# Unread products, later due times and norms on VectorE in an attention layer with masks and residual norms

## The chip, the core and the metric

The kernel runs on one core of one Trainium2 chip. The metric is the time of one execution on the device in microseconds; the time of a kernel is the median of its runs. The engines are called PE (TensorE), DVE (VectorE), ACT (ScalarE), POOL (GpSimd) and SP (SyncE, which here only issues DMAs); PEld is PE's loading of weights.

## The reference

`x` is 8 frames of 2048 nodes with 256 channels, `adj` a 2048 x 2048 matrix of integers; all is float32.

```
def ln(x, g, b): return (x - mean(x)) * rsqrt(var(x) + 1e-5) * g + b      # over the 256 channels
q, k, v  = split(x @ w_qkv)                 # 8 heads of 32 channels
scores   = q . k / sqrt(32);  scores = where(adj > 0, scores, -1e9)
t        = softmax(scores) @ v
x1       = ln(x + t, ln1_g, ln1_b)
h        = relu(x1 @ w1 + b1)
x2       = ln(x1 + h @ w2 + b2, ln2_g, ln2_b)
out      = (x + x2 - mean) / sqrt(var + 1e-5)
```

So every row passes three norms: after attention, after the feed-forward part, and after the outer residual.

## The kernel before

**Items.** The work is a list of 1024 items (L658): 8 frames f, 4 chunks qc of 512 queries, 2 groups g of 4 heads, 16 blocks mb of 128 keys. One step t of the main loop (L733) does, in this order: side jobs (`advance`, L626), the exponential of item t + 1 on ACT (L283), the scores of item t + 2 (L276 on PE, and on DVE the addition of the mask, L279, which moves them from PSUM into a tile `p`), the values product of item t (L310 on PE), and the share of item t in the softmax sums (`add_up`, L324). There are 12 tiles `p`. Scores lie in three pairs of PSUM banks. Of the two other banks one gathers the values of a group, and the other serves the side jobs, one at a time.

**Softmax sums.** The 16 exponentials of a group are added up in three or four chains: some on POOL (L339, 4.9 us each), some by accumulating DMAs that POOL issues (L336); the heads of the chains are then multiplied with ones on PE (`denominator`, L367, product L383 "halves"), one chain head after the other, and may wait for late ones. After the second group the sums are turned (L393) and inverted, and `outcome` (L402) turns the attention output, multiplies it, and has x added by a DMA.

**Tails.** Ten steps later the chunk's `tail` (L435) starts: the first norm, the feed-forward part (`feed_forward`, L571: turn, w1 in two sets of two products, w2 in two), second norm, scale and shift on POOL (L445, L447), addition of x by DMA (L450), third norm, write to `out` (L453). A norm (L344) is statistics on DVE (L348, L349), the root on POOL (L353 to L357) and one activation per 256 channels on ACT (L360). The parameter `per` tells how many of a chunk's four row groups are treated per step. The chunk before the last has x loaded ahead (`xb`): PE adds it (L414), and at the end POOL does (L447).

**The planner.** Side jobs are generators in `fill`, sorted by their due step. A job yields a number of steps to sleep, or BANK before it takes the PSUM bank, or MORE between two sets of products for the same bank (and then keeps the bank). Sets cost credit: 4 x columns each, so 2048 for a set of four products of 512 columns; each step grants 2200, and at most 2200 is kept. `more()` lets a job go on while 1024 of credit is left, or if the due step of a waiting or holding job has been reached:

```
due = [e[3] for e in fill if e[2] == BANK and e[0] <= t or e is state["holder"]]
return finish or state["credit"] >= UNIT or min(due) <= t
```

So a step takes one set, and more than one only if a job is overdue. The other jobs are loading and turning x, the projections to q, k and v of the next frame, and in the first frame the masks.

**The ending.** The last group of the last chunk is done in two halves of 256 queries (L257, L290). `closing(h)` (L473) sums the exponentials of half h (L494), turns sums and attention output, and does the tail of its 256 queries itself: statistics (L456), norms (L467: a small product on DVE, two activations on ACT), feed-forward, norms, write (L569). `closing(0)` is due at step 1024, `closing(1)` at 1023. After the last item the planner runs everything to its end (L778).

After that, a check of all sums (L975 to L988) decides whether a general path is taken; here it isn't.

Of the kernel before, what the change touches and what calls it, by code (L numbers as in the profile page):

```python
# [61 lines left out]
def fast_path(ctx, tc, cst, x, adj, out, RS):  # L62
# [339 lines left out]
    def outcome(f, qc):  # L402
        yield ROOM
        state["tails"] += 1
        xin = x[f, qc * CH:(qc + 1) * CH, :].rearrange("(p j) c -> p j c", p=P)
        y = yp.tile([P, TPC, C], F32, name="y")
        begin = items.index((f, qc, 1, LAST)) + SUM + 2
        yield from divide(f, qc, y)
        if (f, qc) == (F - 1, NCK - 2):
            xb = state["xb"]  # L410
            for j in range(0, TPC, 2):
                yield BANK
                ps = bank()
                columns(ps, ident, xb[:, j:j + 2, :].rearrange("p j c -> p (j c)"), start=True, stop=True)  # L414
                nc.vector.tensor_tensor(y[:, j:j + 2, :], ps.rearrange("p (j c) -> p j c", c=C), y[:, j:j + 2, :], ALU.add)
            start(begin + 4, tail(f, qc, y, xin, 2, xb), begin + 18)
            return
        nc.gpsimd.dma_start(y, xin, accum_op=ALU.add)
        if (f, qc) == (F - 1, NCK - 3):
            start(begin + 10, tail(f, qc, y, xin, 2), begin + 18)  # L420
        else:
            start(begin + 10, tail(f, qc, y, xin), begin + 26)

    def divide(f, qc, y):
        rc = RC.pop((f, qc))
# [9 lines left out]
    def tail(f, qc, y, xin, per=1, xb=None):  # L435
        yield from norm(y, per)
        yield from feed_forward(y)
        if xb is not None:
            nc.gpsimd.tensor_tensor(xb, xb, rows(cst["be2r"]), ALU.add)
        yield 1  # L440
        z = y
        yield from norm(z, per if per == 1 else TPC)
        while xb is None and per > 1 and state["now"] % MB not in CALM:
            yield 1
        nc.gpsimd.tensor_tensor(z, z, rows(cst["g2r"]), ALU.mult)  # L445
        yield 1
        nc.gpsimd.tensor_tensor(z, z, rows(cst["be2r"]) if xb is None else xb, ALU.add)  # L447
        yield 1
        if xb is None:
            nc.gpsimd.dma_start(z, xin, accum_op=ALU.add)  # L450
            yield 7 if per == 1 else 10
        yield from norm(z, per)
        nc.sync.dma_start(out[f, qc * CH:(qc + 1) * CH, :].rearrange("(p j) c -> p j c", p=P), z)  # L453
        state["tails"] -= 1

    def half_stats(t):  # L456
        mv = small.tile([P, 2, nc.vector.BN_AGGR_DIM], F32, name="mv")
        for j in range(2):
            st = small.tile([P, nc.vector.BN_STATS_DIM], F32, name="st")
            nc.vector.bn_stats(st, t[:, j, :])  # L460
            nc.vector.bn_aggr(mv[:, j, :], st)
        rs = small.tile([P, 2], F32, name="rs")
        nc.gpsimd.tensor_scalar(rs, mv[:, :, 1], EPS, 1.0, op0=ALU.add, op1=ALU.mult)
        nc.gpsimd.tensor_tensor(rs, rs, cst["mhalf"][:, 0:2], ALU.pow)
        return mv, rs

    def half_norm(t, mv, rs):  # L467
        nb = small.tile([P, 2], F32, name="nb")
        nc.vector.scalar_tensor_tensor(nb, mv[:, :, 0], -1.0, rs, op0=ALU.mult, op1=ALU.mult)
        for j in range(2):  # L470
            nc.scalar.activation(t[:, j, :], t[:, j, :], AF.Identity, bias=nb[:, j:j + 1], scale=rs[:, j:j + 1])

    def closing(h):  # L473
        f, qc, g = ENDING
        own, part, t0 = slice(2 * h, 2 * h + 2), slice(h * HQ, (h + 1) * HQ), len(items) - MB // 2 * (2 - h)
        terms = [(5, 6), (1, 7), (0, 7), (6, 8), (7, 8)]
        dst = out[f, qc * CH + h * HQ:qc * CH + (h + 1) * HQ, :].rearrange("(p j) c -> p j c", p=P)

        def row2(v):
            return v[:, None, :].to_broadcast([P, 2, C])  # L480

        yield BANK
        ps = bank()
        for n, (block, when) in enumerate(terms):
            if n:
                yield MORE
            while state["now"] < t0 + when:
                yield WAIT
            term = PT.pop((*ENDING, block + h * MB // 2))
            state["credit"] -= 4 * CH  # L490
            for b in range(2):
                for i in range(4):
                    r = D * i
                    nc.tensor.matmul(ps[r:r + D, 0:HQ], cst["halves"][:, g, :], term[:, i, b * HQ:(b + 1) * HQ],  # L494
                                     start=(n + b == 0), stop=(n + b == len(terms)))
        dT = DT[f, qc]
        nc.vector.tensor_tensor(dT[:, part], ps[:, 0:HQ], dT[:, part], ALU.add)
        if h == 0:
            state["y"] = yp.tile([P, TPC, C], F32, name="y")
            state["ff"] = [work.tile([P, 2, CH], F32, name=n) for n in ("turned", "hT")]  # L500
        y, (yT, hT) = state["y"][:, own], state["ff"]
        xr, xb = (t[:, own] for t in state["rows"])
        def turned_sums():
            ps = bank()
            transposes(ps, [dT[:, part][:, j::2] for j in range(2)])
            den = ps[:, 0:HQ].rearrange("p (j c) -> p j c", c=P)[:, :, ::D // 2]
            rc = op.tile([P, 2, H], F32, name="rc")
            nc.vector.reciprocal(rc, den)
            return rc, den

        def count(den):
            nc.vector.tensor_tensor(RS[:, 0, own], RS[:, 0, own], den, ALU.add)
            nc.vector.tensor_tensor(RS[:, 1, own], RS[:, 1, own], den, ALU.min)

        yield 1
        if h == 0:
            yield BANK
            rc, den = turned_sums()
            count(den)
        yield BANK  # L520
        po = bank()
        transposes(po, [OT[f, qc, gg][:, part][:, j::2] for gg in range(2) for j in range(2)])
        if h:
            rc, den = turned_sums()
        for gg in range(2):
            nc.vector.tensor_tensor(y[:, :, gg * P:(gg + 1) * P].rearrange("p j (h d) -> p j h d", d=D),
                                    po[:, gg * HQ:(gg + 1) * HQ].rearrange("p (j h d) -> p j h d", h=4, d=D),
                                    rc[:, :, gg::2, None].to_broadcast([P, 2, 4, D]), ALU.mult)
        nc.vector.tensor_tensor(y, y, xr, ALU.add)
        found = half_stats(y)  # L530
        if h:
            count(den)
        yield 1
        half_norm(y, *found)
        nc.gpsimd.tensor_tensor(xr, y, row2(cst["g1r"]), ALU.mult)
        nc.gpsimd.tensor_tensor(xr, xr, row2(cst["be1b2r"]), ALU.add)
        yield BANK
        ps = bank()
        transposes(ps, [y[:, j, a * P:(a + 1) * P] for a in range(2) for j in range(2)])
        for a in range(2):  # L540
            nc.scalar.activation(yT[:, a, part], ps[:, a * HQ:(a + 1) * HQ], AF.Identity,
                                 bias=cst["be1c"][:, a:a + 1], scale=cst["g1c"][:, a:a + 1])
        yield 1
        for d in range(2):
            yield BANK
            ps = bank()
            for a in range(2):
                columns(ps[:, 0:HQ], w1s[:, a, d * P:(d + 1) * P], yT[:, a, part], start=(a == 0), stop=(a == 1))
            nc.scalar.activation(hT[:, d, part], ps[:, 0:HQ], AF.Relu, bias=cst["b1s"][:, d:d + 1], scale=1.0)
        yield 1  # L550
        yield BANK
        ps = bank()
        for j in range(2):
            if j:
                yield MORE
            for d in range(2):
                columns(ps[:, j * C:(j + 1) * C], hT[:, d, part][:, j * P:(j + 1) * P], w2s[:, d, :], start=(d == 0), stop=(d == 1))
        z = y
        nc.vector.tensor_tensor(z, ps.rearrange("p (b c) -> p b c", c=C), xr, ALU.add)
        found = half_stats(z)  # L560
        yield 1
        half_norm(z, *found)
        yield 1
        nc.vector.tensor_tensor(z, z, row2(cst["g2r"]), ALU.mult)
        nc.vector.tensor_tensor(z, z, xb, ALU.add)
        found = half_stats(z)
        yield 1
        half_norm(z, *found)
        nc.sync.dma_start(dst, z)  # L569
# [40 lines left out]
    def start(t, gen, due):  # L610
        fill.append([t, gen, 1, due])
        fill.sort(key=lambda e: e[3])
# [408 lines left out]
```

## Time and profile before

| | |
|---|---|
| median of 3 runs | 3159.01 us (3158.67 to 3160.27) |
| profiled execution | 3158.02 us |
| its span, first to last instruction | 3156.0 us |
| mean granted PE clock | 0.994 |
| busy: PE / DVE / POOL / ACT | 97% / 87% / 86% / 77% |
| exponential of 128 x 2048 (L283) | 1.910 us |
| mask addition of 128 x 1024 (L279), two per step | 1.218 us |
| POOL addition of 128 x 2048 (L339) | 4.890 us |
| DMAs: accumulating p (L336), issue to landing | 9.1 us median, 7.0 to 15.5 |

All times inside the run are microseconds from the first instruction of the span. In a row of the timeline the first number is the start, the second the time to the end of the last instruction that the row takes together, x the number of instructions (PE executes each float32 product as two), and in brackets stands the idle time of the engine before it and what ended it. A group's row shows line, engine, operation, output and inputs, their shapes, the count, then total busy time in us and the mean in ns, and the idle time before with its causes. The granted clock is the share of PE's full clock.

### The profile page before, as it was taken

The numbers are of one execution on the slowest core, as the hardware profiler recorded it, in microseconds if no ns is written. First come the engines' busy times: TensorE is split into PE (matmuls) and PEld (weight loads), VectorE is DVE, ScalarE is ACT, GpSimd is POOL, SyncE is SP. The second block draws the span as 40 slices with busy tenths as digits, with TensorE's granted clock in tenths as the row PEclk, the third lists the DMA queues.
The fourth block names the chain that finished last, engine by engine and source line by source line (L and its number), as shares of the span: only waits on it lengthen the run. The fifth ranks groups of instructions, "written<-read, shape, count | busy, mean of one in ns | idle before, by whom it ended". The sixth has DMA issues, their size and how long they took to land.

```text
span 3156.0 us, 68508 instructions
## 1 busy us (share of the span) xinstructions
PE 3051.3 (97%) x28988; PEld 962.6 (31%) x28988; DVE 2747.6 (87%) x3139; ACT 2427.1 (77%) x1934; POOL 2727.7 (86%) x1389
## 2 busy tenths in 40 slices
PE   8999999999999999999999999999999999999986
PEld 4222333233332233223332323323333233322223
DVE  4989888998888988888988888988888988889885
ACT  4877878777778877778777878778778778778774
POOL 1768989888889888899888899899989899899985
PEclk9999999999999999999999999999999999999998
DMA  8998878889789888789878899788888889778871
GB/s 258 223 210 185 196 170 194 193 191 198 173 174 209 197 190 178 170 195 214 192 169 187 187 207 195 166 184 204 197 176 191 190 192 202 167 173 166 173 157 42
DMA packets 165465, 586.86 MB, mean 186 GB/s; under 512 B 15360, under 2 KB 84480, under 8 KB 116512
## 3 DMA queue, kind: packets, MB, share of 16 engines
q0 software_dynamic: 63696, 430.60, 69.4%
q1 hardware_dynamic: 100640, 150.50, 14.1%
q8 instruction: 229, 3.75, 0.5%
q10 hardware_dynamic: 816, 1.31, 0.1%
q14 instruction: 84, 0.69, 0.1%
HBM read 146.15 MB, written 37.75 MB: 58 GB/s over the span
## 4 chain that ended last, share of the span: by engine, by line


## 5 line engine op out<-in xcount | busy, mean ns | idle before, releaser
L279 DVE TENSOR_TENSOR p<-s,mask 128x1024 f32<-128x1024 f32 x2016 | 2371.5, 1218 | 297.7 <-PE s L276 123.4
L283 ACT ACTIVATE p<-p 128x2048 f32<-128x2048 f32 x1024 | 1955.7, 1910 | 551.1 <-DVE p L279 449.1
L339 POOL TENSOR_TENSOR p<-p 128x2048 f32<-128x2048 f32 x409 | 1999.9, 4890 | 221.3 <-ACT p L283 200.4
L276 PE MATMUL s<-qT,kT 32*128 32x512 f32 x8064 | 1152.0, 640 | 56.5 <-DVE p L279 52.6
L310 PE MATMUL x<-p,v 128*32 128x512 f32 x8064 | 1075.8, 606 | 5.8 <-ACT p L283 4.2
L276 PEld LDWEIGHTS s<-qT,kT 32*128 32x128 f32 x8064 | 315.3, 183 | 659.5 <-DVE p L279 629.4
L336 POOL DMA_DIRECT2D p<-p x378 | 416.2, 1104 | 49.2 <-ACT p L283 41.0
L310 PEld LDWEIGHTS x<-p,v 128*32 128x32 f32 x8064 | 158.7, 108 | 771.3 <-issue 315.1
L54 PE MATMUL x<-in,wqkv 128*32 128x512 f32 x1888 | 245.7, 592 | 0.0
L383 PE MATMUL x<-p,halves 128*32 128x512 f32 x1768 | 231.1, 594 | 1.6 <-DVE kT L170 1.4
L360 ACT ACTIVATE y<-y,nb,rs 128x256 f32<-128x256 f32 x372 | 218.3, 591 | 0.5 <-POOL nb L357 0.5
L348 DVE BATCH_NORM_STATS2 st<-y 128x6 f32<-128x256 f32 x372 | 154.8, 416 | 0.0
L54 PE MATMUL x<-turned,w1s 128*32 128x512 f32 (+1 forms) x1008 | 125.2, 593 | 0.0
L54 PEld LDWEIGHTS x<-wqkv,in 128*32 128x32 f32 x3584 | 102.4, 110 | 66.5 <-issue 55.4
L54 PE MATMUL x<-w2s,hT 128*32 128x256 f32 x2048 | 122.0, 379 | 0.0
L54 PE MATMUL x<-wqkv,in 128*32 128x128 f32 x3584 | 118.2, 273 | 0.0
L54 PEld LDWEIGHTS x<-in,wqkv 128*32 128x32 f32 x1888 | 61.3, 110 | 141.3 <-issue 116.0
L354 POOL TENSOR_TENSOR rs<-rs,mhalf 128x4 f32<-128x4 f32 x93 | 96.2, 1035 | 7.8
L445 POOL TENSOR_TENSOR y<-y,g2r 128x1024 f32<-128x1024 f32 x31 | 99.3, 3205 | 2.2 <-ACT y L360 2.2
L383 PEld LDWEIGHTS x<-p,halves 128*32 128x32 f32 x1768 | 57.3, 110 | 133.9 <-issue 126.5
L447 POOL TENSOR_TENSOR y<-y,be2r 128x1024 f32<-128x1024 f32 x30 | 94.4, 3145 | 0.2
L54 PEld LDWEIGHTS x<-w2s,hT 128*32 128x32 f32 x2048 | 66.4, 110 | 69.7 <-issue 35.6
(164 smaller groups left out, 1433.6 us busy)
## 6 DMA issues: line engine op xcount, KB each, us to landing
p<-p POOLq DMA_DIRECT2D x380, 1024.0 KB, 9.1
in<-xd SPq DMA_DIRECT2D x87, 512.0 KB, 7.5
mask<-md SPq DMA_DIRECT2D x248, 128.0 KB, 5.4
y<-in_x_dram POOLq DMA_DIRECT2D x60, 512.0 KB, 10.3
out_dram<-y SPq DMA_DIRECT2D x31, 512.0 KB, 4.5
in<-in_x_dram SPq DMA_DIRECT2D x30, 512.0 KB, 6.8
xd<-in SPq DMA_DIRECT2D x28, 512.0 KB, 6.8
p<-in_adj_dram SPq DMA_DIRECT2D x8, 1024.0 KB, 14.3
```

The costliest lines, as they stand in the source:

```text
L54: nc.tensor.matmul(out[r:r + D], lhsT[:, r:r + D], rhs, start=start, stop=stop)
L276: nc.tensor.matmul(ps2[half][:, j, :], KT[f, mb // TPC, g][r:r + D, (mb % TPC) * P:(mb % TPC + 1) * P], QT[f, qc, g][r:r + D, :], start=Tr ...
L279: nc.vector.tensor_tensor(pt[:, 2 * half:2 * half + 2, :], ps, MK[f, qc, mb // 2][:, mb % 2, None, :].to_broadcast([P, 2, CH]), ALU.add)
L283: nc.scalar.activation(PT[item], PT[item], AF.Exp, scale=1.0 / math.sqrt(D))
L310: nc.tensor.matmul(O[grp][r:r + D, :], V[f, mb // TPC, g][:, mb % TPC, r:r + D], PT[item][:, h, :], start=(mb == 0), stop=(mb == LAST))
L336: nc.gpsimd.dma_start(PT[f, qc, g, chain[0]], PT.pop(item), accum_op=ALU.add)
L339: nc.gpsimd.tensor_tensor(first, first, PT.pop(item), ALU.add)
L348: nc.vector.bn_stats(st, t[:, j, :])
L354: nc.gpsimd.tensor_tensor(rs, rs, cst["mhalf"], ALU.pow)
L360: nc.scalar.activation(t[:, j, :], t[:, j, :], AF.Identity, bias=nb[:, j:j + 1], scale=rs[:, j:j + 1])
L383: nc.tensor.matmul(ps[r:r + D, :], cst["halves"][:, g, :], term[:, h, :], start=(n == 0), stop=(n == len(blocks) - 1))
L445: nc.gpsimd.tensor_tensor(z, z, rows(cst["g2r"]), ALU.mult)
```

## The change

It has five parts, all in the code quoted above.

1. Tails are due 30 instead of 26 steps after their sums; the tail of the chunk before the last is due 14 instead of 18 steps after, and its last norm takes all four row groups per step and one yield less.
2. Half norms (`half_norm`) are done by DVE alone: one tensor_scalar (subtract mean, multiply by the root) per 256 channels instead of a small product on DVE and activations on ACT.
3. In `closing(0)`, behind the turned output, five sets of four products of 512 columns go into a bank that nobody reads.
4. In `closing`, the two products on POOL that prepare the residual come after the activations of the turned rows.
5. In `closing`, scale and shift behind the second norm are taken together with the norm: (z - mean) * g2 and then * root + xb, one scalar_tensor_tensor each per 256 channels, and only the second needs the root.

In the orders of the built programs `closing(1)` comes ahead of `closing(0)` in the end; before the change it was the other way round.

```diff
-            start(begin + 4, tail(f, qc, y, xin, 2, xb), begin + 18)
+            start(begin + 4, tail(f, qc, y, xin, 2, xb), begin + 14)
...
-            start(begin + 10, tail(f, qc, y, xin), begin + 26)
+            start(begin + 10, tail(f, qc, y, xin), begin + 30)
...
         nc.gpsimd.tensor_tensor(z, z, rows(cst["g2r"]), ALU.mult)
-        yield 1
+        if xb is None:
+            yield 1
         nc.gpsimd.tensor_tensor(z, z, rows(cst["be2r"]) if xb is None else xb, ALU.add)
...
-        yield from norm(z, per)
+        yield from norm(z, per if xb is None else TPC)
...
     def half_norm(t, mv, rs):
-        nb = small.tile([P, 2], F32, name="nb")
-        nc.vector.scalar_tensor_tensor(nb, mv[:, :, 0], -1.0, rs, op0=ALU.mult, op1=ALU.mult)
         for j in range(2):
-            nc.scalar.activation(t[:, j, :], t[:, j, :], AF.Identity, bias=nb[:, j:j + 1], scale=rs[:, j:j + 1])
+            nc.vector.tensor_scalar(t[:, j, :], t[:, j, :], mv[:, j, 0:1], rs[:, j:j + 1], op0=ALU.subtract, op1=ALU.mult)
...
         if h:
             rc, den = turned_sums()
+        else:
+            again = bank()
+            for n in range(5):
+                columns(again, ident, OT[f, qc, 0], start=True, stop=True)
...
         half_norm(y, *found)
-        nc.gpsimd.tensor_tensor(xr, y, row2(cst["g1r"]), ALU.mult)
-        nc.gpsimd.tensor_tensor(xr, xr, row2(cst["be1b2r"]), ALU.add)
...
         yield 1
+        nc.gpsimd.tensor_tensor(xr, y, row2(cst["g1r"]), ALU.mult)
+        nc.gpsimd.tensor_tensor(xr, xr, row2(cst["be1b2r"]), ALU.add)
...
-        found = half_stats(z)
-        yield 1
-        half_norm(z, *found)
-        yield 1
-        nc.vector.tensor_tensor(z, z, row2(cst["g2r"]), ALU.mult)
-        nc.vector.tensor_tensor(z, z, xb, ALU.add)
+        mv, rs = half_stats(z)
+        for j in range(2):
+            nc.vector.scalar_tensor_tensor(z[:, j, :], z[:, j, :], mv[:, j, 0:1], cst["g2r"], op0=ALU.subtract, op1=ALU.mult)
+        yield 1
+        for j in range(2):
+            nc.vector.scalar_tensor_tensor(z[:, j, :], z[:, j, :], rs[:, j:j + 1], xb[:, j, :], op0=ALU.mult, op1=ALU.add)
```

## The prediction

> **What bounds the kernel now.** I read the shares of busy time first, then the waits, then PE's timeline in the middle and the timeline of all engines over the last 50 us; the page's own chain is empty for this run.
>
> ```profile
> PE 3051.3 (97%) x28988; PEld 962.6 (31%) x28988; DVE 2747.6 (87%) x3139; ACT 2427.1 (77%) x1934; POOL 2727.7 (86%) x1389
> L279 DVE TENSOR_TENSOR p<-s,mask 128x1024 f32<-128x1024 f32 x2016 | 2371.5, 1218 | 297.7 <-PE s L276 123.4
> ```
>
> PE is nearly full, DVE comes next with two mask additions of 1.218 us per step. The waits name no engine that PE waits for over more than 53 us in all. So the middle is read step by step, from one values group (L310) to the next:
>
> ```profile
> 2825.02 1.06 PE L310 MATMUL x<-p,v 128*32 128x512 f32 x8
> 2825.90 1.91 PE L54 MATMUL x<-w2s,hT 128*32 128x256 f32 x32
> 2828.81 1.07 PE L310 MATMUL x<-p,v 128*32 128x512 f32 x8
> ...
> 2832.61 1.07 PE L310 MATMUL x<-p,v 128*32 128x512 f32 x8
> 2833.49 1.04 PE L383 MATMUL x<-p,halves 128*32 128x512 f32 x8
> 2835.53 1.07 PE L310 MATMUL x<-p,v 128*32 128x512 f32 x8
> ```
>
> ```profile
> 2864.72 1.06 PE L310 MATMUL x<-p,v 128*32 128x512 f32 x8
> 2866.21 1.14 PE L276 MATMUL s<-qT,kT 32*128 32x512 f32 x8 [0.42 <-DVE p L279]
> 2867.28 1.06 PE L310 MATMUL x<-p,v 128*32 128x512 f32 x8
> ```
>
> A step with two sets of side products (w2s, x32) takes 2828.81 - 2825.02 = 3.79 us, with one set (halves) 2.92, with none 2.56. A set costs 3.79 - 2.92 = 0.87 when PE is the bound; the empty step is held by DVE (the 0.42 wait) and wastes 2.56 - (2.92 - 0.87) = 0.51. So a second set in a step is bad only because elsewhere a step then stands empty. Steps that hold only transposes take 2.65 to 2.8, up to 3.2 where DVE turns a chunk's sums.
>
> The end, after the last exponential (its end is 3112.24; I call it E), is a chain through all engines:
>
> ```profile
> 3112.30 1.07 PE L298 MATMUL x<-p,v 128*32 128x256 f32 x16 [1.66 <-ACT p L283]
> 3113.18 4.50 PE L494 MATMUL s<-p,halves 128*32 128x256 f32 x80
> ...
> 3130.46 1.94 PE L54 MATMUL x<-turned,w1s 128*32 128x256 f32 x16
> 3132.17 4.42 PE L54 MATMUL s<-turned,w1s 128*32 128x256 f32 x48
> 3138.49 0.69 DVE L559 TENSOR_TENSOR y<-x,in 128x512 f32<-128x512 f32 x1 [11.85 <-PE x L54]
> 3150.03 1.09 ACT L471 ACTIVATE y<-y,nb,rs 128x256 f32<-128x256 f32 x2 [0.19 <-DVE nb L469]
> ```
>
> Five sets of sums follow the last values; the sums' addition on DVE starts at E+5.5 (3117.75), w1s at E+18.2, the first addition of w2s's result at E+26.25, the last activation ends at E+38.9, the span at E+43.8. By stretches of 3.41 us (columns: length, then PE, PEld, DVE, ACT, POOL busy, granted clock, DMA share, GB/s):
>
> ```profile
> 3118.45:3121.86 3.41, 0.87 (x8) 0.68 (x6) 3.12 (x11) 0.00 (x0) 0.36 (x2) 1.00 0.00 0
> 3121.86:3125.27 3.41, 0.00 (x0) 0.00 (x0) 3.21 (x13) 0.00 (x0) 0.53 (x1) 0.50 0.00 0
> 3128.69:3132.10 3.41, 2.94 (x20) 1.48 (x24) 0.00 (x0) 1.91 (x4) 2.95 (x3) 0.50 0.00 0
> 3132.10:3135.51 3.41, 3.41 (x36) 1.58 (x32) 0.00 (x0) 0.95 (x2) 1.79 (x5) 0.50 0.02 5
> ```
>
> While DVE normalizes, PE stands still for 6.8 us and its clock is halved, so w1s's four blocks run at half speed: 1.7 us each instead of the 0.86 that equally wide blocks took at E.
>
> **Due times (tails four steps later).** A set is only placed twice in a step when a job is overdue. I counted sets per step in both built programs' order of PE instructions (steps 1 to 1010, before the last chunk's end); a set is four products of 512 columns or as much in narrower ones:
>
> empty 67 to 47; transposes only 227 to 227; one set 625 to 672; two 91 to 57; three 0 to 7. Sets in all: 625 + 182 = 807 and 672 + 114 + 21 = 807.
>
> With 2.56, 2.92, 3.79 and 3.79 + 0.87 = 4.66: -20 x 2.56 + 47 x 2.92 - 34 x 3.79 + 7 x 4.66 = -51.2 + 137.2 - 128.9 + 32.6 = **-10.3 us**. Bounds: 0, if DVE holds the newly filled steps, to -13 (some removed empty steps cost 2.8). I take the sum: masks need 2.44 of 2.92 us, and one norm's statistics per step (0.57) already stand in runs of steps at 2.92 to 2.94.
>
> The three-set steps are new: in frames 1 to 7 the sums of a group end in one step, 3 steps later than before. Until then their buffers of the 12 exponential tiles stay taken, and the next mask addition reuses a tile 2 steps after its accumulating DMA was issued, where 5 or 6 were usual. At the place in question (frame 2) that DMA starts 0.8 us after its step's values and lands 7.8 later, at 8.6; over the six such places 7.3 to 9.5. The addition comes due at 2 x 2.92 + 4.66 + 0.2 = 10.7. I cost the wait at 0; its bounds are 0 and, with the line's longest landing (15.5), 5.6 us seven times. POOL's additions (4.6 to 4.9 us) fit with 3 us to spare.
>
> **Last steps (1011 to E).** The last full tail is due four steps earlier, so its sums stand three in a step, and two more sets of the ending's halves come ahead of E: over these steps +4.66 + 2 x 2.94 - 3 x 2.92 = +1.8. Against this, the tail's four activations (2.06 us, which stood in front of the last exponential and held it to 3110.35) come two steps earlier, where ACT has over 1 us of slack a step: -0.8. Sum **+1.0** (0 to +2).
>
> **From E to w1s.** Three of the five sets moved ahead: 3 x 0.86, so the sums' addition starts at E+2.9 instead of E+5.5. The tail's last statistics now precede it on DVE and wait for POOL's L448 (about E+0.9); with 2.1 us of statistics DVE is free at E+3.0, so this costs 0.1, and every microsecond POOL is later would cost one. From there, by rows of before: addition 0.43, transposes and semaphores 0.65, reciprocal 0.25, two products 0.76, addition 0.69, statistics 1.08; second half's reciprocal and both halves' counting 0.75, products 0.78, reductions 0.2, addition 0.69, checks 0.1, statistics 1.08; two norms of the first half 0.6; POOL's root for the second ends 1.1 after its statistics, so 0.5 is left; two norms 0.6; transposes 0.6. Together 9.8: w1s starts at E+12.8 (before: E+18.2). The norm as tensor_scalar 128x256 on DVE has no row; L526's 0.38 a piece is above it, a quarter of L700's 0.691 (128x1024) below; I take 0.3. POOL's four products (1.27 each), now behind the roots, end at E+16.2 and are needed at E+18.3. On SP the tail's write now stands ahead of the check's load and of the two last writes; those come due much later, so I cost it at 0.
>
> The unread products, 5 x 0.87 = 4.3, stand behind all transposes on PE: from E+4.9 to E+9.2. The first norm arrives at E+10.8, so nothing waits for them. Idle is left for 1.6 us. The emptiest stretch of 3.41 us then holds about 1.4 of PE work, 0.42. In the trace such stretches with 0.26, 0.31, 0.35 and 0.39 were followed by half clock, those with 0.49 and more were not. I take full clock: w1s 4 x 0.86 = 3.4 instead of 5.96, w2s at E+16.2. If the clock falls, up to 1.7 us is lost.
>
> The Trainium skill ("TensorE: Matmul & The Clock Gate", Part 1) lets the clock fall after an idle window of about 3.4 us, which would make 0.42 safe beyond doubt; the stretch with 0.87 of 3.41 busy, followed by half clock, is stricter than that, and by it the case is near the edge. By the page the sum is 3140, by the row 3140 to 3142.
>
> **From w2s to the end.** The addition follows w2s's start by 2.07: E+18.3 (before E+26.25). From then DVE does all: two additions 1.42, four statistics 4.32, eight scalar_tensor_tensor 128x256 (no row; L526's 0.38, L564's half 0.34) 3.04, four norms 1.2, the check 0.3, and 0.5 of POOL's last root uncovered: 10.8, against 12.63 before. End of work E+29.1, and 4.9 to the span's end as before: E+34.0 against E+43.8, **-9.8** (-7.5 to -11).
>
> **Sum.** -10.3 + 1.0 - 9.8 = -19.1. The profiled execution took 3158.02 (span 3156.0): 3138.9. The median of the runs shown lies 1.0 above it: **3140** us.
>
> **Rivals.**
> - *DVE takes the filled steps over* (20%): the -10.3 is gone, the end remains: 3150. For it: DVE is 87% busy, and 0.69 additions (L605) now stand in steps of 2.92 instead of 3.79. Against it: two masks and all of a tail's DVE work (11 us per 32 steps) make 89 of 93 us.
> - *The clock falls anyway* (10%): 3142. For it: if DVE's norms take 0.43 the gap grows by 0.5 and the emptiest stretch falls under 0.39.
> - *Slower, through tiles* (4%): the accumulating DMA at the three-set step lands late in each of seven frames. Free up to a landing of 9.9 us, it eats the whole gain from 9.9 + 19.1/7 = 12.6 on; at 15.5 the time is 3140 + 39 = 3179. Against it: 7.3 to 9.5 at these places.
> - *The products are not there or do not hold the clock*: they are in the built program (20 products), so this is the second rival.
>
> **Numbers.** Forecast 62% (3135 to 3145), the rivals 20, 10 and 4, something else 4. The range 3135 to 3147 takes in the forecast, the clock rival and part of the first. What the measurement can tell from no change is 0.2%, 6.3 us: forecast, first and second rival are faster, with half of the rest same: faster 0.92, same 0.04, slower 0.04.
>
> **What would show it.** Values to values 2.92 where a w2s set stands alone; 57 steps at 3.79 and seven at 4.66; the sums' addition on DVE at E+2.9, w1s at E+12.8 with 0.86 a block and clock 1.00, the span's end at E+34. Wrong would be steps of one set at over 3.0 (DVE), a mask addition waiting for a DMA in steps 22 to 24 of a frame, or half clock in w1s.

## The result, and the profile after

The changed kernel takes **3151.78 us** (median of 12 runs, 3150.16 to 3155.2), the kernel before, run beside it, 3159.06 (12 runs, 3156.55 to 3160.61): ratio 0.9979, 95% interval 0.9972 to 0.9987. It is faster by 7.3 us, where 19.1 were forecast.

The profiled execution of the changed kernel has a span of 3153.2, that of before 3156.0. The 2.8 between them are not the effect, since the start differs by 4.65: the first values group (step 0) begins at 68.50 us in the record after and at 63.85 in that of before. No edit acts ahead of it, and in the records below it lies anywhere from 64.8 to 68.5. So I compare from step 0 on, which gives -7.4, what the medians give too:

| stretch | forecast | after - before, us |
|---|---|---|
| step 0 to step 128 (frame 0) | | -4.84 |
| step 128 to 896 (frames 1 to 6) | | -0.29 |
| step 896 to 1010 | | +3.88 |
| steps 0 to 1010 together | -10.3 | **-1.25** |
| step 1010 to E (end of the last exponential) | +1.0 | +1.04 |
| E to the span's end | -9.8 | **-7.20** |
| sum | -19.1 | -7.4 |

Records of kernels with the same sets per step differ by up to 0.8 over steps 0 to 1010 (before 3006.32 and e2 3005.53; the changed kernel 3005.06 and e4 3004.27), so the middle's -1.25 is little more than that.

The busy shares say nothing of this. The lines of the page after (engines, and the costliest group with its mean ns and its idle time):

```profile
PE 3057.3 (97%) x29028; PEld 963.5 (31%) x29028; DVE 2749.5 (87%) x3145; ACT 2416.9 (77%) x1922; POOL 2727.7 (87%) x1389
...
L279 DVE TENSOR_TENSOR p<-s,mask 128x1024 f32<-128x1024 f32 x2016 | 2371.5, 1218 | 310.3 <-PE s L276 133.1
```

DVE's additions cost the same 1.218 us, PE is as full as before. PE's timeline of the record after, where the tail's sets stand:

```profile
2829.26 1.07 PE L310 MATMUL x<-p,v 128*32 128x512 f32 x8
2830.14 1.04 PE L54 MATMUL x<-turned,w1s 128*32 128x512 f32 x8
...
2832.18 1.07 PE L310 MATMUL x<-p,v 128*32 128x512 f32 x8
2833.06 1.90 PE L54 MATMUL x<-turned,w1s 128*32 128x512 f32 x16
...
2835.96 1.06 PE L310 MATMUL x<-p,v 128*32 128x512 f32 x8
```

From values to values 2.92 with one set and 3.78 with two: the lengths are those forecast. Averaged over steps 1 to 1010, by what PE does beside scores and values:

| step holds | before: steps, mean us | after: steps, mean us | difference of the sums |
|---|---|---|---|
| nothing | 67, 2.744 | 47, 2.807 | -51.9 |
| one set | 625, 2.942 | 672, 2.939 | +136.4 |
| two sets | 91, 3.790 | 57, 3.793 | -128.7 |
| three sets | 0 | 7, 4.642 | +32.5 |
| transposes of the sums (dT) | 31, 2.957 | 31, 3.032 | +2.3 |
| transposes of the rows (oT) | 62, 2.876 | 62, 2.999 | +7.6 |
| other transposes | 134, 2.75 | 134, 2.76 | +0.6 |

The first four rows make -11.7, the forecast's -10.3 and a little more. **The transposing steps, which I had counted as "227 to 227", became longer by 10.5 and took it back.** The place is easy to see once one looks at DVE. VectorE's timeline around the turning of one chunk's sums (frame 3, last chunk), before:

```profile
1513.15 0.68 DVE L389 TENSOR_TENSOR dT<-x,dT 128x512 f32<-128x512 f32 x1
1513.81 2.35 DVE L279 TENSOR_TENSOR p<-s,mask 128x1024 f32<-128x1024 f32 x2
1516.08 0.35 DVE L396 RECIPROCAL rc<-x 128x32 f32<-128x32 f32 x1
...
1518.84 0.68 DVE L431 TENSOR_TENSOR y<-x,rc 128x512 f32<-128x512 f32 x1
```

PE's timeline of the same steps, before:

```profile
1513.61 1.06 PE L310 MATMUL x<-p,v 128*32 128x512 f32 x8
1514.61 0.75 PE L95 MATMUL x<-ident,dT 128*128 128x128 f32 x4
1515.29 1.14 PE L276 MATMUL s<-qT,kT 32*128 32x512 f32 x8
1516.36 1.06 PE L310 MATMUL x<-p,v 128*32 128x512 f32 x8
...
1519.10 1.06 PE L310 MATMUL x<-p,v 128*32 128x512 f32 x8
```

And the same stretch after, DVE and then PE:

```profile
1512.84 0.68 DVE L389 TENSOR_TENSOR dT<-x,dT 128x512 f32<-128x512 f32 x1
1513.43 0.42 DVE L348 BATCH_NORM_STATS2 st<-y 128x6 f32<-128x256 f32 x1
...
1513.99 2.36 DVE L279 TENSOR_TENSOR p<-s,mask 128x1024 f32<-128x1024 f32 x2
1516.26 0.42 DVE L348 BATCH_NORM_STATS2 st<-y 128x6 f32<-128x256 f32 x1
...
1519.46 0.68 DVE L431 TENSOR_TENSOR y<-x,rc 128x512 f32<-128x512 f32 x1
```

```profile
1513.29 1.06 PE L310 MATMUL x<-p,v 128*32 128x512 f32 x8
1514.29 0.74 PE L95 MATMUL x<-ident,dT 128*128 128x128 f32 x4
1515.27 1.14 PE L276 MATMUL s<-qT,kT 32*128 32x512 f32 x8 [0.23 <-DVE p L279]
1516.34 1.06 PE L310 MATMUL x<-p,v 128*32 128x512 f32 x8
...
1518.46 1.14 PE L276 MATMUL s<-qT,kT 32*128 32x512 f32 x8 [0.33 <-DVE p L279]
1519.54 1.06 PE L310 MATMUL x<-p,v 128*32 128x512 f32 x8
```

Between the sums' addition (L389) and the first division (L431) DVE works without a gap in both. Before, that is 5.69 us; after, 6.62, since two of the four statistics of an older tail's second norm now stand in between. PE has only transposes there and waits for DVE (0.23, 0.33): the dT step and the two oT steps behind it take 3.05, 3.20 and 2.86 where they took 2.75, 2.74 and 2.75. The statistics come four steps later because their tail does.

The end after (timeline of all engines; PE is ready for the second half's transposes at 3128.3):

```profile
3127.02 0.70 DVE L470 TENSOR_SCALAR y<-y,mv,rs 128x256 f32<-128x256 f32 x2
...
3127.55 0.78 PE L95 MATMUL s<-ident,y 128*128 128x128 f32 x4 [1.46 <-DVE y L470]
...
3128.25 1.26 POOL L545 TENSOR_TENSOR in<-y,g1r 128x512 f32<-128x512 f32 x1
3128.32 2.69 DVE L470 TENSOR_SCALAR y<-y,mv,rs 128x256 f32<-128x256 f32 x2 [0.59 <-POOL rs L465]
...
3129.59 1.26 POOL L546 TENSOR_TENSOR in<-in,be1b2r 128x512 f32<-128x512 f32 x1
...
3131.06 0.79 PE L95 MATMUL x<-ident,y 128*128 128x128 f32 x3 [0.95 <-DVE y L470]
...
3131.78 1.93 PE L54 MATMUL x<-turned,w1s 128*32 128x256 f32 x16
...
3136.65 3.63 PE L54 MATMUL x<-w2s,hT 128*32 128x256 f32 x64
```

The same instruction, L470, takes 0.70 for the first half's two pieces and 2.69 for the second's, while POOL multiplies the residual. That puts w1s at E+15.1 (E is 3116.67) instead of the forecast E+12.8. And PE's clock falls after all; by stretches of 3.41 us (PE, PEld, DVE, ACT, POOL busy, granted clock, DMA share, GB/s):

```profile
3127.82:3131.23 3.41, 0.98 (x7) 0.58 (x7) 2.69 (x2) 1.02 (x2) 3.10 (x4) 1.00 0.00 0
3131.23:3134.64 3.41, 3.41 (x31) 1.58 (x34) 0.00 (x0) 1.50 (x3) 2.39 (x2) 0.50 0.02 5
```

A stretch with 0.98 of 3.41 busy (0.29) is followed by one at half clock, and w1s takes 4.87 instead of 3.4.

### The profile page after: what moved, and what is told of

Read it like the earlier page. It is cut to its first block, busy times and chain, and to the rows that moved or that the text cites. A ratio compares the mean times of both kernels' runs of the same rounds, so it can differ in the third digit from the quotient of the medians.

```text
span 3153.2 us, 68635 instructions
## 1 busy us (share of the span) xinstructions
PE 3057.3 (97%) x29028; PEld 963.5 (31%) x29028; DVE 2749.5 (87%) x3145; ACT 2416.9 (77%) x1922; POOL 2727.7 (87%) x1389
## 5 line engine op out<-in xcount | busy, mean ns | idle before, releaser
L339 POOL TENSOR_TENSOR p<-p 128x2048 f32<-128x2048 f32 x409 | 1954.8, 4780 | 231.9 <-ACT p L283 227.6
L336 POOL DMA_DIRECT2D p<-p x378 | 381.9, 1013 | 67.6 <-ACT p L283 53.3
L348 DVE BATCH_NORM_STATS2 st<-y 128x6 f32<-128x256 f32 x372 | 154.8, 416 | 3.2 <-POOL y L448 3.2
L445 POOL TENSOR_TENSOR y<-y,g2r 128x1024 f32<-128x1024 f32 x31 | 92.2, 2973 | 0.0
L448 POOL TENSOR_TENSOR y<-y,be2r 128x1024 f32<-128x1024 f32 x30 | 78.7, 2625 | 1.1
```

Source lines behind the costliest of these rows:

```text
L336: nc.gpsimd.dma_start(PT[f, qc, g, chain[0]], PT.pop(item), accum_op=ALU.add)
L339: nc.gpsimd.tensor_tensor(first, first, PT.pop(item), ALU.add)
```

## The experiments

Two questions were open. For the middle: **theory A**, the place of the statistics makes the transposing steps longer; against it, **B**, that the turning steps keep their lengths, so that the due times do bring 10 and the end nothing, and **B'**, that the spread sets themselves hold DVE. For the end: **theory P**, VectorE's norm is held up by GpSimd's products; against it, that the norm waited for something else (Q). Each run was compared with runs of the kernel before on the same chip (medians 3159.05, 3158.75 and 3159.54 for the three groups of runs):

| run | median us | ratio to before, 95% interval |
|---|---|---|
| e1_due_only | 3158.9 | 1.0000, 0.9991 to 1.0009 |
| e2_end_only | 3153.57 | 0.9983, 0.9974 to 0.9992 |
| e4_pool_later | 3148.88 | 0.9969, 0.9958 to 0.9980 |
| x1_before_hold3 | 3166.84 | 1.0024, 1.0014 to 1.0033 |
| x2_turn_later_34 | 3177.78 | 1.0065, 1.0051 to 1.0079 |
| x3_turn_later_26 | 3147.37 | 0.9964, 0.9951 to 0.9978 |
| x4_no_products | 3151.09 | 0.9976, 0.9967 to 0.9985 |
| x5_norm_stt | 3153.66 | 0.9981, 0.9972 to 0.9990 |
| x8_norm_act | 3154.02 | 0.9985, 0.9976 to 0.9994 |
| x6_six_products | 3148.85 | 0.9965, 0.9951 to 0.9979 |
| x7_turn_six | 3145.98 | 0.9959, 0.9945 to 0.9973 |

**e1: the due times alone**, in the kernel before.

```diff
-            start(begin + 10, tail(f, qc, y, xin), begin + 26)
+            start(begin + 10, tail(f, qc, y, xin), begin + 30)
```

> The kernel before with the later due time of the full tails (26 to 30) alone. Theory A (collision): the sets of side products are spread as forecast (-10.3 by the step counts), but the second norm's statistics now fall on the steps in which DVE turns the next chunk's sums, where PE has only transposes, and these steps get longer by about 10 in all: 3159.0 - 1 = 3158 us, with dT steps at 3.03, oT steps at 3.00 and in-steps at 2.76 in place of 2.96, 2.88 and 2.73. The forecast (B): these steps keep their lengths, 3159 - 10 = 3149 us; the missing gain of the changed kernel would then lie in its end.

Measured 3158.9, ratio 1.0000: the due times bring nothing that can be measured. dT steps take 3.033, oT steps 3.000, other transposes as after; the sets stand exactly as after. The forecast's 3149 is out.

**e2: the end alone**, the changed kernel with `begin + 26`.

> The changed kernel with the full tails' due time back at 26: the changes of the end alone. Theory A: the due times bring only about 1 us, so 3151.8 + 1 = 3153 us, -6 against before. Theory B: the due times bring 10, so the end brings nothing and this kernel takes 3159 or more. The record of the changed kernel's end (values of the last step to the span's end 36.2 in place of 43.7 us, 1.3 lost in the last steps) speaks for -6.

Measured 3153.57, -5.5 against before. So the gain of the change is that of its end; the 1.8 us by which it stays behind the changed kernel are within what the two intervals leave open. In the records 1.1 of it lies behind E: in e2's, PE is at half clock for two stretches, from 3126.75 to 3133.57, in the changed kernel's for one.

**x1: the collision alone.** The kernel before, in which a full tail's second norm waits at the beginning of a pair of groups:

```diff
         z = y
+        while per == 1 and state["now"] % (2 * MB) in (0, 1, 2):
+            yield 1
         yield from norm(z, per if per == 1 else TPC)
```

> The kernel before, with its due times, but a tail's second norm starts its statistics no earlier than three steps into a pair of groups (waits in steps 0 to 2): the statistics' four steps then fall on the steps in which DVE turns the next chunk's sums, in every chunk, and no set of PE's products moves. Theory A (collision): the dT steps go to about 3.05, the oT steps to 3.2 (one of two) and the step behind to 2.86, together +6 to +10 us: 3165 to 3169. Theory B' (the spreading of the sets itself slows DVE's steps, since the 3.79-us steps that let DVE catch up are gone): nothing is spread here, so 3159.

Measured 3166.84, +7.8 (interval +4.4 to +10.4). The counts of sets per step are those of before to the last one, and so are their lengths (one set 2.938, two 3.790); dT steps go from 2.957 to 3.026, oT steps from 2.876 to 2.947, together +6.5, and frames 1 to 6 take 6.2 more. Nothing was spread here, so B' falls: the second norm's statistics, moved by a few steps with no work added, lengthen the turning.

Why +6.5 here and +9.9 in the changed kernel shows when the 31 turnings (a dT step and the two oT steps behind it) are counted by how many of the tails' statistics (L348, 0.42 each, and L349, 0.18) begin on DVE in the dT step:

| statistics in the dT step | the three steps, us | before | after (e1 and e4 the same) | x1 | x3 |
|---|---|---|---|---|---|
| none | 2.74, 2.74, 2.75 | 10 | 3 | 2 | 30 |
| one | 3.08, 2.74, 2.78 | 7 | 0 | 8 | 0 |
| two | 3.05, 3.19, 2.86 | 14 | 28 | 21 | 1 |

The lengths are means of the record of before; those of the other records differ by 0.03 at most, but for one turning of x1. A turning with two statistics is 0.87 longer than one with none, with one 0.37 longer. So 21 of the turnings were hit before the change already, 7 of them by one statistic only. 14 more with two, at 0.87, and 7 fewer with one, at 0.37, make +9.6 of the +9.9. x1 by the same prices: 7 x 0.87 + 0.37 = +6.5. x3 (below) against e4: -27 x 0.87 = -23.5, measured -24.

**e4: POOL's products of the closing behind both halves' norms.**

```diff
-        nc.gpsimd.tensor_tensor(xr, y, row2(cst["g1r"]), ALU.mult)
-        nc.gpsimd.tensor_tensor(xr, xr, row2(cst["be1b2r"]), ALU.add)
+        if h == 0:
+            both = [(state["rows"][0][:, 2 * i:2 * i + 2], state["y"][:, 2 * i:2 * i + 2]) for i in range(2)]
+            for i in (0, 1):
+                nc.gpsimd.tensor_tensor(both[i][0], both[i][1], row2(cst["g1r"]), ALU.mult)
+            for i in (1, 0):
+                nc.gpsimd.tensor_tensor(both[i][0], both[i][0], row2(cst["be1b2r"]), ALU.add)
```

> The changed kernel with POOL's four products of the closing (g1, be1b2) behind both halves' first norms: the second half's product first, so that none starts before its norm is done. Theory P (VectorE's norm and GpSimd's product hold each other up): the second half's two norms take 0.70 in place of 2.69 us, its transposes come 2.0 earlier, w1s at E+12.8 in place of E+14.8, w1s itself runs at full clock (3.4 instead of 4.9): -2 to -3.5 us, 3148 to 3150. Rival Q (the norm waited for its root, or a single slow execution): the two norms still take 2.69, no gain: 3152.

Measured 3148.88, -10.2 against before and about -3 against the changed kernel; the two intervals overlap, but from E to the span's end the records differ by as much (33.25 and 36.52). Its end, all engines:

```profile
3125.84 0.73 DVE L470 TENSOR_SCALAR y<-y,mv,rs 128x256 f32<-128x256 f32 x2 [0.59 <-POOL rs L465]
...
3126.65 2.51 POOL L548 TENSOR_TENSOR in<-y,g1r 128x512 f32<-128x512 f32 x2 [0.85 <-DVE y L470]
...
3127.10 1.07 PE L54 MATMUL x<-turned,w1s 128*32 128x256 f32 x16
...
3130.58 3.64 PE L54 MATMUL x<-w2s,hT 128*32 128x256 f32 x64
```

The norm waits for the same root just as long (0.59) and then takes 0.73 instead of 2.69. w1s starts at E+13.2, runs at full clock in 3.48, and from E to the span's end it is 33.25 us. In e2's record, with POOL's products where the change has them, the second norm takes 2.69 again, so it was no single slow execution. P holds, Q falls.

**x5: another instruction for the norm**, POOL's products where the change has them.

```diff
-            nc.vector.tensor_scalar(t[:, j, :], t[:, j, :], mv[:, j, 0:1], rs[:, j:j + 1], op0=ALU.subtract, op1=ALU.mult)
+            nc.vector.scalar_tensor_tensor(t[:, j, :], t[:, j, :], mv[:, j, 0:1], rs[:, j:j + 1].to_broadcast([P, C]), op0=ALU.subtract, op1=ALU.mult)
```

> The changed kernel with the halves' norm written as scalar_tensor_tensor, (y - mean) * root with the root as a broadcast row, in place of tensor_scalar with two scalars; POOL's products stay where the change put them. Theory P1 (only tensor_scalar on float32 in SBUF is shut out while POOL's product runs): the second half's two norms take about 0.85 (as the record's other scalar_tensor_tensor, 0.42 each) in place of 2.69 us, w1s comes 1.8 earlier, and the time is 3149 to 3150.5; each undisturbed norm costs 0.07 more. Theory P2 (any VectorE norm beside POOL's product is held up): still about 2.6 us, 3152.

Measured 3153.66. P1 falls:

```profile
3128.29 2.88 DVE L470 SCALAR_TENSOR_TENSOR y<-y,mv,rs 128x256 f32<-128x256 f32 x2 [0.59 <-POOL rs L465]
```

This form, too, is held up while POOL's products run (3128.23 to 3129.49 and 3129.57 to 3130.89): its two pieces take 1.48 each, undisturbed ones 0.45 to 0.48.

**x8: the halves' norms back on ScalarE** (the old `half_norm` in the changed kernel).

> The changed kernel with the halves' norms back on ScalarE (the old half_norm: -mean*root on DVE, two activations). By the forecast's step the norm on VectorE is worth 0.5 to 0.8 each time it stands on the path (first half, second half, last half): +2, 3153.5 to 3154. By theory P the second half's norm costs 2.69 on VectorE here, and the activations (1.09 and 0.3 ahead of them) are shorter than that: first half +0.7, second half -1.3, last half +0.7: 3152, no difference.

Measured 3154.02, +2.2 against the changed kernel, as the forecast's step had it; the two intervals overlap. In the records the second half's norm ends at E+14.31 on ScalarE and at E+14.34 on VectorE, and w1s starts at E+15.2 and E+15.1. Until w1s the change's "norms by VectorE alone" brought nothing, because POOL's products stood beside one of them. From w1s to w2s x8 takes 5.84 against 4.87, with half clock over two stretches in place of one. From w2s to the span's end it is 17.9 against 16.5: 0.5 of this up to the end of the last norm, 0.85 behind it, where the last write lands 3.28 us after its issue instead of 2.33. The joined scale and shift are in both kernels, so x8 does not price them.

**x4: without the unread products**, in e4's kernel (it leaves out the five sets that nothing reads).

> The kernel with POOL's late products (e4) without the five sets of unread products. The forecast's step (the products hold the clock): PE then stands still from E+4.9 to E+10.8 but for transposes, the clock is halved for one or two stretches from about E+10, w1s takes up to 5.1 in place of 3.4 us and the end comes 1.7 to 2.5 later: 3150.6 to 3151.5. Rival: the transposes alone hold the clock, or w1s is not on the path: 3149.

Measured 3151.09, +2.2 against e4; the two intervals overlap, and in the records it is +2.34 from E to the span's end. Its record has half clock from E+7.5 over three stretches, and w1s takes 5.5 in place of 3.48. The first two of them and the one ahead:

```profile
3120.58:3123.99 3.41, 1.16 (x9) 0.96 (x8) 2.76 (x9) 2.04 (x4) 1.17 (x3) 1.00 0.00 0
3123.99:3127.40 3.41, 0.00 (x0) 0.00 (x0) 3.34 (x18) 0.03 (x1) 1.02 (x3) 0.50 0.38 154
3127.40:3130.82 3.42, 3.08 (x16) 1.77 (x20) 1.15 (x4) 1.70 (x4) 2.49 (x4) 0.50 0.00 0
```

This step of the forecast is right in size.

**x6: six sets of products** in e4's kernel (`range(6)`).

> The kernel with POOL's late products (e4) with six in place of five sets of unread products: PE's gap ahead of the first half's transposes falls from 1.47 to 0.6 us, nothing waits for the sixth. Theory E (the clock is near its edge with five: held in one record, halved in another, by where the 3.41-us windows fall): the median falls by 0.3 to 1.2, 3147.7 to 3148.6, with w1s at full clock in the record. Rival: five are enough, 3148.9.

Measured 3148.85: no difference that can be measured against e4. What the sixth does shows only in records: e4's emptiest stretch there is 1.95 of 3.41 busy (0.57), with six it is 0.82. x3 (below) has the same end as e4 with five sets, and its record shows the edge; e4's stretch and the next first, then x3's:

```profile
3121.65:3125.06 3.41, 1.95 (x20) 0.41 (x13) 3.34 (x16) 0.00 (x0) 1.06 (x4) 1.00 0.38 154
3125.06:3128.48 3.42, 2.86 (x36) 1.74 (x40) 0.92 (x3) 2.28 (x5) 2.57 (x3) 1.00 0.02 5
```

```profile
3119.70:3123.11 3.41, 1.53 (x12) 0.45 (x4) 2.75 (x11) 0.38 (x1) 1.01 (x2) 1.00 0.30 119
3123.11:3126.53 3.42, 3.29 (x28) 1.76 (x32) 0.31 (x1) 1.88 (x5) 2.95 (x3) 0.50 0.02 5
```

The gap of 1.5 us is the same; in x3 it lies within a stretch that is busy for 1.53 (0.45), and w1s took 4.55. Where the stretches fall differs from one execution to the next: one begins at E+7.8 in e4's record and at E+8.7 in x3's.

**x2 and x3: the turning moved out of the statistics' way**, on top of e4: the transposes of the sums wait three steps longer, and the tails start later.

```diff
         nc.vector.tensor_tensor(dT, ps, dT, ALU.add)
-        yield 1
+        yield 4 if (f, qc) < (F - 1, NCK - 3) else 1
...
-            start(begin + 10, tail(f, qc, y, xin), begin + 30)
+            start(begin + 14, tail(f, qc, y, xin), begin + 34)    # x2
+            start(begin + 12, tail(f, qc, y, xin), begin + 26)    # x3
```

> The kernel with POOL's late products (e4), and the turning of a chunk's sums three steps later (the wait behind the sums' addition 4 in place of 1 step, except in the last two chunks), the full tails started and due four steps later (begin + 14, begin + 34). The second norm's statistics now end before the turning begins. Theory A (collision): the dT steps fall from 3.03 to about 2.75 and the oT steps from 3.00 to 2.80-2.85, -18 us over their 93; the sets stand a little worse (by the order of PE's instructions 89 steps empty, 595 with one set, 85 with two, 14 with three: at 2.61, 2.93, 3.79 and 4.64 +11 against e4). Sum -5 to -12: 3137 to 3144 us. Theory B' (spread sets hold DVE, the place of the statistics doesn't matter): dT and oT steps stay at 3.0, and the worse sets show in full: 3160.

> As the run before with the tails started two steps later and due as before the change (begin + 12, begin + 26). The sets stand about as in the kernel before (76 empty, 607 with one, 100 with two), and the statistics fall ahead of the turning. Theory A: dT and oT steps at 2.75 and 2.83, against e4 about -18 from these and +10 from the sets: 3139 to 3146 us, so that the later due time would not be needed at all. Theory B': sets as before, 3.79-us steps back, transposes as in the kernel before (2.96, 2.88): about e4 + 1 = 3150.

x2 is slower than anything else here, 3177.78 (its profiled execution, 3173.36, is the fastest of five), and yet theory A's part came as expected: dT steps 2.751, oT steps 2.764 (e4: 3.034, 3.000), together -23. Two things ate it. My +11 for the sets was a slip: the same counts and lengths give 42 x 2.61 - 77 x 2.93 + 28 x 3.79 + 7 x 4.64 = +22.6. And two waits are new, of which the record of after has none:

```profile
DVE p L279 <- DMA p<-p: 19.7, 14, 3.2
...
DVE st L348 <- DMA y<-in_x_dram: 11.9, 9, 1.9
```

(total us, times, longest). The first is the wait of the forecast's "slower" rival, tile reuse: a mask addition does wait for an accumulating DMA. Only 3 of its 14 cases (8.4 us) come one step after a three-set step, of which frames 1 to 6 have twelve here instead of six; most of the others stand at steps 74 to 76 of a frame, away from any such step, and why the DMA is late there stays open. The second is a tail started before its rows had landed. With these waits in them, the steps with sets and the empty ones come to +34.8 against e4, the other transposes to +11; frames 1 to 6 are 18.3 longer than e4's.

x3 has 3147.37, -1.5 against e4 and inside its interval. In the record dT and oT steps are at 2.753 and 2.754, -24 over the 93 steps as A has it, and the older due time's sets cost +21.5 (my +10 was a slip as well, +15.7 by its own counts). Frames 1 to 6 alone are 6.1 shorter. A is confirmed; as a gain it is small, since each arrangement pays with sets what it saves in turning.

**x7: all that helped**, x3 with six sets of products.

> All that helped together: POOL's late products, the later turning of the sums with tails at begin + 12 and due at begin + 26, and six sets of unread products. Theories A, P and E add: 3147.4 - (0.3 to 1.2) = 3146.2 to 3147.1 us. If the turning's gain was only one kernel's luck: 3148 to 3149.

Measured 3145.98, ratio 0.9959 (0.9945 to 0.9973): the fastest, below both kernels; its interval overlaps those of e4 and x3. From E to the span's end it is 33.2, w1s at full clock.

## Why the prediction was wrong

The direction was right, the size was not: 7.3 of 19.1, outside the range. By its steps:

- **Due times, "transposes only 227 to 227".** This is the term that failed. The number of steps is right, the tacit assumption that they keep their lengths is not: +10.5, nearly all in the 93 steps of dT and oT (+9.9). I had read that these steps take "up to 3.2 where DVE turns a chunk's sums" and not asked which of them do: the ones with a tail's statistics in them, 14 turnings with two before and 28 after, at 0.87 each. The counts of the other steps are right and their lengths nearly so (-11.7 for -10.3; two sets 3.793 forecast 3.79, three 4.642 forecast 4.66, one 2.939 forecast 2.92; empty steps take 2.74 before and 2.81 after, but the 20 that went took 2.60 on average, priced at 2.56). e1 measured the whole edit at nothing, x1 showed the cause by itself, x2 and x3 its reverse.
- What I left out is a part of every move: I followed what a later tail does to PE, and not where its DVE instructions land. The bound "0, if DVE holds the newly filled steps" held the number and the first rival (20%, 3150) was the nearest case, but it named the wrong steps: filled steps stayed at 2.93 to 2.94, the turning ones grew.
- In frame 0 the edit gains 4.84 and in the last steps it loses 3.88. Sets in steps 1 to 128 fall from 79 to 73, in steps 897 to 1010 they rise from 76 to 82: the later due time carries six sets (5.2 us at 0.87) from one into the other. Frames 1 to 6, with 652 sets in both, are the edit's own account: -8.7 for sets and empty steps, +8.4 for transposes.
- **Tile reuse costed at 0**: right for this change (no such wait in the record), and a real edge: x2 crosses it, though mostly not at the three-set steps where I looked for it.
- **Last steps +1.0**: +1.04.
- **E to w1s.** The sums' addition at E+3.3 (forecast 2.9; it waits for the statistics and these for POOL's L448, which ended at E+1.14). w1s at E+15.1, forecast 12.8: of the 2.3 the stretched second norm is 2.0. In e4, x6 and x7, without it, w1s starts at E+12.9 to 13.2. The step that failed is "POOL's four products (1.27 each), now behind the roots": I asked when they end, not what they do to DVE while they run. L470 alone takes 0.38 to 0.41 a piece, two in 0.70 (0.3 each was taken).
- **Clock.** The products do what they were costed for (x4: 2.2), and yet the second rival (10%, the clock falls) came true, because the late norm emptied the stretch ahead of w1s to 0.29: +1.4. The bound I took from before, half clock up to 0.39 and full from 0.49, holds roughly: between 0.45 and 0.50 both happen. Stretches of 0.45 (x3, at 3119.70), 0.48 (changed kernel, at 55.81) and 0.50 (x2, at 3145.38) were followed by half clock, one of 0.45 (changed kernel, at 3052.72) was not; the busy share alone does not decide there. The Trainium skill ("TensorE: Matmul & The Clock Gate", Part 1) ties the fall to an idle window; the stretches of 0.29 and 0.45 show that a half-filled one is enough, so the measurement decides.
- **From w2s to the end.** 10.8 of DVE work was forecast, 10.9 measured (3138.69 to 3149.59); scalar_tensor_tensor 0.47 a piece instead of 0.38, the norms a little more, the rest less. From there to the span's end 3.6, not 4.9: the last write lands 2.33 after its issue, in before 3.67. That is 1.3 better than costed and nothing I had forecast; why the write lands sooner stays open.

With e4's placement the end is 33.25, -10.5 against before's 43.7, and the forecast was -9.8; without the earlier landing of the last write, which was luck, it would be about -9.2. The plan of the end was sound but for the one collision.

## What to carry to other kernels

When a job moves, list its instructions on every engine at the place where they land, not only on the engine that is full: a step with little for PE is where DVE's extra 0.6 us becomes the bound. Count steps by their kind and price each kind by the neighbours it will have afterwards, since "unchanged" steps are where a gain goes. And where a VectorE tensor_scalar or scalar_tensor_tensor on SBUF is on the path, do not start a float32 GpSimd operation beside it.

## What the runs showed of the hardware

- While POOL ran a float32 tensor_tensor in SBUF (128x512, 1.26 us), VectorE's tensor_scalar (128x256 in SBUF, 0.38 to 0.41 alone) took 1.34 and 1.42, scalar_tensor_tensor (0.45 to 0.48 alone) 1.48: each ended 0.15 to 0.29 after POOL's operation did. It is shown as VectorE's busy time, not as a wait. Two other kinds are not touched: in the record of the changed kernel 1240 mask additions with an operand in PSUM that ran beside POOL's float32 additions and products (for four fifths of their time or more) took 1.218, the 261 free ones 1.219, and 289 statistics 0.416 (free 0.415).
- The Trainium skill has this ("SBUF — State Buffer", section "Who interferes with whom"): a pair of ports shared by the two engines is locked for a whole instruction, against a VectorE operation with two inputs in SBUF or in its two-port mode. All rows above agree with it, x5's included, though none shows which mode tensor_scalar ran in; the page would have told against the place of the products.
- The same end, gap and products had full clock in e4's record and half in x3's (w1s 3.48 and 4.55): the granted clock goes by stretches of 3.41 us whose place differs between executions, and the gap's stretch was 0.57 busy in one and 0.45 in the other.
